# Top-16 attention on one Trainium2 core: the sixteen largest of a row found by way of fifteen groups, with one pool of two accumulator banks and another order of the loop

## The chip, the cores and the metric

The kernel runs on one core of one Trainium2 chip. The time is the device time of one execution in microseconds (us). Three runs of the kernel before gave 1539.97, 1541.5 and 1545.21 us; the median is 1541.5 us. Durations below come from one further execution, which was profiled.

The core has five engines that run their own instruction streams in order and wait for each other by semaphores: PE (matrix products, into PSUM banks), DVE (VectorE), ACT (ScalarE), POOL (GpSimd) and SP, which starts DMAs.

## What is computed

The reference is a small graph network on 1250 nodes with 512 channels: a graph layer, an attention with experts, a second graph layer, and a second attention. Each adds to the node features. Only the second attention is touched here. Cut to what matters, for each of 8 heads (m = 1250 rows, 64 channels a head):

```python
logits = jnp.einsum('bmd,bpd->bmp', q * scale, k)   # 8 x 1250 x 1250
_, idx = lax.top_k(logits, 16)                      # the sixteen largest of each row
attn = softmax(logits at idx)                       # over these sixteen alone
out = attn @ (v at idx)                             # then the output product wo
```

Each row of 1250 scores needs its sixteen largest. The kernel gathers nothing. It finds the sixteenth largest score of each row, forms exp of all scores, and multiplies by the sign of (score minus a limit just under the sixteenth). The negative products are later cut off at zero, so only the sixteen remain.

## The kernel before: how the second attention is staged

The 1250 rows are ten row tiles of P = 125 rows. A step n is one row tile i and one pair j of heads; a_ = 0 or 1 says which head of the pair. So there are 40 steps, four to a row tile, and 80 heads-of-a-tile, called heads below. The whole loop is recorded with a schedule written out by hand: each helper puts its instructions at the end of its engine's stream, and the order of the calls is the order on each engine. A semaphore wait is added wherever a tile is read or reused.

What a head goes through, with the lines of the kernel before:

- `scores1` (L1592): six matmuls write the score tile S of 125 x 1250 float32. S takes three PSUM banks, and each of the two heads of a pair has one S (two pools of three banks). The next step's matmuls for the same a_ wait until the S of this step has been read for the last time.
- `first1` (L1606 to L1609): DVE's MAX8 instruction gives the eight largest of S. POOL then makes nm (minus the largest) and gap (a small distance), by three one-column instructions.
- `without1` (L1617): DVE's MATCH_REPLACE8, with the load of its eight values, copies S to `rest` in SBUF with those eight put out.
- `second1` (L1626, L1627): MAX8 over `rest` gives the ninth to the sixteenth, and POOL makes `below`, the limit, with one more one-column instruction.
- `weights1` (L1634): ACT writes e = exp(S + nm). `select1` (L1641, L1644): ACT writes the sign sg of (S + below), with a sum over the row, and POOL multiplies e by sg in place. This multiplication of 125 x 1250 elements is called **the product** below; both of its inputs are in SBUF. The sign is the last reader of S.
- One step later `turn1` (L1654) and `keep1` (L1661): five groups of four transposes on PE into a PSUM bank, each copied by ACT to SBUF with negative values cut to zero.
- Two steps later `values1` (L1710), `outputs1` (L1720): forty small matmuls with the values v, and ACT's copy of the result.
- By row tile: `halves1` splits the next tile's queries (ACT L1577, POOL L1578, two DMAs on SP), in two of the four steps. `sums1`, `sums_exp1`, `sums_over1`, `sums_wide1`, `sums_turn1`, `sums_keep1` and `scale1` form the sums of the sixteen exponentials and scale the output of the tile before (POOL L1670, L1684 and L1698 among them). `project1` (L1728) and `finish1` (L1736, L1738) are the output product, the addition to the node features and the DMA out.

PSUM has eight banks here: six for the two S, one for the transposes (pool ps_t1) and one for everything else that PE writes (pool ps_o1).

At the end the row sums of the signs are compared with N - 32. If a row did not select exactly sixteen, the whole result is computed again by a slower general program that stands behind it.

Of the kernel before, what the change touches and what calls it, by code (L numbers as in the profile page):

```python
# [9 lines left out]
F32 = mybir.dt.float32  # L10
# [562 lines left out]
def tile_usual(ctx: ExitStack, tc: tile.TileContext, a: dict, out: bass.AP):  # L573
# [968 lines left out]


    TINY = 2.0 ** -22
    wo_pool, wo_p = pool("wo", 1)
    w_o = wo_p.tile([128, K, D], F32, name="w_o1")
# [3 lines left out]
    with (  # L1550
        tc.tile_pool(name="att1", bufs=2, side="right", reuse_waits="tile") as at1,
        tc.tile_pool(name="ps_t1", bufs=1, space=PSUM) as ps_t1,
        tc.tile_pool(name="ps_o1", bufs=1, space=PSUM) as ps_o1,
        tc.tile_pool(name="ps_s1b", bufs=1, space=PSUM) as ps_s1b,
        tc.tile_pool(name="ps_s1a", bufs=1, space=PSUM) as ps_s1a,
    ):
        ps_s1 = (ps_s1a, ps_s1b)
        w_v = at1.tile([128, K, D], F32, name="w_v1b", bufs=1)
        v_b = at1.tile([P, D], F32, name="v_b1b", bufs=1)
        signs = at1.tile([P, T * H], F32, name="signs", bufs=1)  # L1560
        steps = [(i, j) for i in range(T) for j in range(K)]
        last = len(steps) - 1
        score, found, bests, es, pTs, outs, turned = {}, {}, {}, {}, {}, {}, {}

# [17 lines left out]
        def scores1(n, a_, *chunks):  # L1582
            if n > last:
                return
            i, j = steps[n]
            h = 2 * j + a_
            if (n, a_) not in score:
                score[n, a_] = ps_s1[a_].tile([P, 3 * 512], F32, name="S")
            for c in chunks:
                n0, n1 = c * 512, min(c * 512 + 512, N)  # L1590
                for x in range(2):
                    nc.tensor.matmul(score[n, a_][:, n0:n1], stacks[i][:, x, h, :], K2[:, h, n0:n1],  # L1592
                                     start=(x == 0), stop=(x == 1))


        def first1(n, a_):
            if n > last:
                return
            i, j = steps[n]
            h = 2 * j + a_  # L1600
            if h == 0:
                bests[i] = at1.tile([P, H, TOPK], F32, name="best")
            top = bests[i][:, h, :]
            nm = at1.tile([P, 1], F32, tag=f"nm{a_}", name="nm1")
            gap = at1.tile([P, 1], F32, tag=f"gap{a_}", name="gap")
            nc.vector.max(out=top[:, 0:8], in_=score[n, a_][:, :N])  # L1606
            nc.gpsimd.tensor_scalar(nm, top[:, 0:1], -1.0, None, op0=ALU.mult)
            nc.gpsimd.tensor_scalar(gap, top[:, 7:8], -1.0, top[:, 0:1], op0=ALU.mult, op1=ALU.max)
            nc.gpsimd.tensor_scalar(gap, gap, TINY, None, op0=ALU.mult)  # L1609
            found[n, a_] = (nm, gap, top)  # L1610

        def without1(n, a_):
            if n > last:
                return
            nm, gap, top = found[n, a_]
            rest = at1.tile([P, N], F32, name="rest", bufs=1)
            nc.vector.match_replace(out=rest, in_to_replace=top[:, 0:8], in_values=score[n, a_][:, :N],  # L1617
                                    imm_value=LOWEST)
            found[n, a_] = (nm, gap, top, rest)

        def second1(n, a_):
            if n > last:
                return
            nm, gap, top, rest = found[n, a_]
            below = at1.tile([P, 1], F32, tag=f"below{a_}", name="below")
            nc.vector.max(out=top[:, 8:16], in_=rest)  # L1626
            nc.gpsimd.tensor_scalar(below, top[:, 15:16], -1.0, gap, op0=ALU.mult, op1=ALU.add)  # L1627
            found[n, a_] = below

        def weights1(n, a_):  # L1630
            if n > last:
                return
            e = at1.tile([P, N], F32, tag=f"e{a_}", name="e")
            nc.scalar.activation(e, score[n, a_][:, :N], AF.Exp, bias=found[n, a_][0])  # L1634
            es[n, a_] = e

        def select1(n, a_):
            if not 0 <= n <= last:
                return
            sg = at1.tile([P, N], F16, tag=f"sg{a_}", name="sg", bufs=1)  # L1640
            nc.scalar.activation(sg, score.pop((n, a_))[:, :N], AF.Sign, bias=found.pop((n, a_)),  # L1641
                                 accum_out=signs[:, 2 * n + a_ : 2 * n + a_ + 1])
            e = es[n, a_]
            (nc.vector if 2 * n + a_ == 2 * last + 1 else nc.gpsimd).tensor_mul(e, e, sg)  # L1644

        def turn1(n, g):
            if not 0 <= n <= last:
                return
            if g == 0:
                pTs[n] = at1.tile([P, 2 * T, P], F32, name="pT1")  # L1650
            turned[n, g] = ps_t1.tile([128, 512], F32, tag="t", name="ps_t1")
            g0, g1 = GROUPS[g]
            for b in range(g0, g1):
                nc.tensor.transpose(turned[n, g][:P, span(b - g0, b - g0 + 1)],  # L1654
                                    es[n, b // T][:, span(b % T, b % T + 1)], ident[:P, :P])
# [31 lines left out]
        def sums_turn1(i):  # L1687
            turned[i] = ps_t1.tile([128, 512], F32, tag="t", name="ps_t1")
            rb = sums.pop(i)
# [10 lines left out]
        def values1(n, t0, t1):  # L1700
# [3 lines left out]
            if t0 == 0:  # L1704
                outs[n] = ps_o1.tile([128, 512], F32, tag="o", name="O")
            pT = pTs[n]
# [15 lines left out]
        def project1(i, c, width=D // K, y=None):  # L1722

            if y is None:
                y = ps_o1.tile([128, 512], F32, tag="o", name="O")[:P, :width]
            cols = slice(c * width, (c + 1) * width)
# [14 lines left out]
        def values_late1(t):  # L1741
            ps = ps_o1.tile([128, 512], F32, tag="o", name="ps_v1")
            value_product1(ps[:P], t, w_v)
            lates.append((t, ps))
# [6 lines left out]
        def signs_over1():  # L1751
# [5 lines left out]
            nc.vector.tensor_copy(worst[:, 1:2], edges)  # L1757
            ps = ps_o1.tile([128, 512], F32, tag="o", name="ps_w1")[:1, :2]
            nc.tensor.matmul(ps, ones, worst, start=True, stop=True)
# [7 lines left out]
        with tc.manual_schedule():  # L1767
            nc.sync.dma_start(w_v, a["qkv"][:, 2 * D :].rearrange("(k p) f -> p k f", p=128))
            nc.sync.dma_start(v_b, bass.AP(tensor=a["v_b"].tensor, offset=a["v_b"].offset, ap=[[0, P], [1, D]]))
            for a_ in range(2):  # L1770
                halves1(0, a_)
            scores1(0, 0, 2, 0, 1)
            for n in range(len(steps)):


                i, c = n // K - 1, n % K
                if i >= 0 and c == 1:
                    sums_over1(i)
                first1(n, 0)
                values1(n - 2, 0, 5)  # L1780
                select1(n - 1, 1)
                turn1(n - 1, 0)
                values1(n - 2, 5, 8)
                keep1(n - 1, 0)
                without1(n, 0)
                if n == 1:
                    keep_late1()
                scores1(n, 1, 2, 1, 0)
                if n < 2:
                    values_late1(T - 3 + 2 * n)  # L1790
                if n <= last and c < 2:
                    halves1(steps[n][0] + 1, c)
                weights1(n, 0)
                turn1(n - 1, 1)
                values1(n - 2, 8, T)
                keep1(n - 1, 1)
                second1(n, 0)
                outputs1(n - 2)
                if i >= 0:
                    if c == 0:  # L1800
                        sums1(i)
                    if c == 1:
                        sums_wide1(i)
                    if c == 2:
                        sums_turn1(i)
                        sums_keep1(i)
                    if c == 3:
                        scale1(i)
                first1(n, 1)
                select1(n, 0)  # L1810
                turn1(n - 1, 2)
                if i >= 1:
                    project1(i - 1, c)
                scores1(n + 1, 0, 2)
                keep1(n - 1, 2)
                if i >= 0 and c == 0:
                    sums_exp1(i)
                if n == 0:
                    keep_late1()
                without1(n, 1)  # L1820
                turn1(n - 1, 3)
                keep1(n - 1, 3)
                scores1(n + 1, 0, 0, 1)
                if n == 0:
                    values_late1(T - 2)
                weights1(n, 1)
                turn1(n - 1, 4)
                keep1(n - 1, 4)
                second1(n, 1)
                if n == 1:  # L1830
                    keep_late1()
                finish1()

# [6 lines left out]
            turn1(n - 1, 0)  # L1840
            values1(n - 2, 5, 8)
            keep1(n - 1, 0)
            sums_exp1(i)
            turn1(n - 1, 1)
            values1(n - 2, 8, T)
            keep1(n - 1, 1)
            outputs1(n - 2)
            sums_over1(i)
# [92 lines left out]
```

## Time and profile before

| What | Value |
|---|---|
| median of three runs | 1541.5 us |
| the profiled execution's own time | 1539.01 us |
| its span in the trace | 1537.1 us |
| first and last MAX8 over S (L1606) | start at 1109.4 and 1506.0 us |
| length of four steps (one row tile), L1606 at 1271.53 to 1311.92 us | 40.39 us |
| busy in the span: PE, DVE, ACT, POOL | 1431.5, 898.1, 707.3, 424.8 us |

The span is the time from the first to the last recorded instruction; the execution's own time is 1.9 us longer. Busy time is the time in which an engine worked on an instruction; matmuls are pipelined and their ends are modelled, so a busy PE is not a PE at its peak. Engine times in a row of groups are the duration of one instruction on its engine. An instruction can begin before the one ahead of it on the same engine has ended, so the distance from start to start can be shorter than the duration.

### The profile page before, as it was taken

To read this page: it belongs to the slowest core of one execution; us is meant where nothing else is said; L and a number is where in the kernel's file an instruction comes from. 1 tells how busy PE (TensorE), PEld (TensorE's weight loads), DVE (VectorE), ACT (ScalarE), POOL (GpSimd) and SP (SyncE) were. 2 spreads that over 40 slices of the span, in tenths; PEclk is the share of its full clock that TensorE was granted. 3 is DMA by queue.
4 is the path that set the end of the run, shared out by engine and by line. 5 is a ranking of instruction groups with operands and counts; after the bars stand their busy time and mean duration, and the time that the engine had idled before them with its cause. 6 is when DMAs were issued, how large, how long until landed. Compare 5 with 4: busy or idle time off the path is not lost.

```text
span 1537.1 us, 21430 instructions
## 1 busy us (share of the span) xinstructions
PE 1431.5 (93%) x8127; PEld 934.1 (61%) x8127; DVE 898.1 (58%) x1412; ACT 707.3 (46%) x1351; POOL 424.8 (28%) x621
## 2 busy tenths in 40 slices
PE   6999999978999998999999999989888999999997
PEld 4557744457778766444444446654466777777775
DVE  8895567544443332422222435653588998999894
ACT  3333444455555552210000223431278888888884
POOL 1110000011111120000000112210168787887873
PEclk9999999989999999999999999999999999999999
DMA  4001000010101010200001100000200000000000
GB/s 138 29 1 55 1 0 1 6 46 14 42 18 48 22 26 17 79 28 28 28 28 41 42 28 1 5 23 0 78 11 14 14 22 21 22 21 22 21 8 23
DMA packets 42323, 41.12 MB, mean 27 GB/s; under 512 B 25738, under 2 KB 30084, under 8 KB 42211
## 3 DMA queue, kind: packets, MB, share of 16 engines
q1 hardware_dynamic: 42211, 39.66, 8.9%
q8 instruction: 66, 1.08, 0.3%
q14 instruction: 46, 0.38, 0.1%
HBM read 26.81 MB, written 2.56 MB: 19 GB/s over the span
## 4 chain that ended last, share of the span: by engine, by line
PE 69%; DVE 13%; ACT 11%; issue 3%; POOL 2%; DMA 0%; ACTq 0%; SPq 0%; DVEq 0%; POOLq 0%
PE ps_o L1334 9%; PE ps_mm L1326 7%; PE S L1592 5%; PE ps_mm L865 5%; PE ps_t L1654 5%; PE ps_mm L800 5%; PE S L1034 4%; PE ps_mm L1462 4%; PE ps_o L870 4%; PE ps_t L1122 4%; PE O L1143 3%; PE O L1710 3%; ACT sg L1641 3%; PE bank L768 2%; PE O L1187 2%
## 5 line engine op out<-in xcount | busy, mean ns | idle before, releaser
L1644 POOL TENSOR_TENSOR e<-e,sg 125x1250 f32<-125x1250 f32 x79 | 203.5, 2576 | 35.0 <-ACT sg L1641 34.1
L1336 DVE SCALAR_TENSOR_TENSOR X<-ps_o,gate,X 125x512 f32<-125x512 f32 x80 | 60.0, 750 | 177.0 <-PE ps_o L1334 177.0
L1592 PE MATMUL S<-K,stacks 128*125 128x512 f32 (+1 forms) x480 | 123.9, 382 | 29.6 <-ACT sg L1641 25.4
L1654 PE MATMUL ps_t<-ident,e 125*125 125x125 f32 x800 | 132.3, 288 | 11.8 <-ACT R L1695 6.7
L1334 PE MATMUL ps_o<-we,hid 128*125 128x512 f32 x320 | 141.2, 595 | 0.0
L1661 ACT ACTIVATE pT<-ps_t 125x500 f32<-125x500 f32 x200 | 118.1, 590 | 50.1 <-PE ps_t L1654 49.2
L1606 DVE MAX8 best<-S 125x8 f32<-125x1250 f32 x80 | 117.0, 1462 | 32.9 <-PE S L1592 32.0
L1654 PEld LDWEIGHTS ps_t<-ident,e 125*125 125x125 f32 x800 | 105.6, 187 | 47.9 <-ACT pT L1661 27.4
L1329 ACT ACTIVATE hid<-ps_mm,b 128x500 f32<-128x500 f32 (+1 forms) x40 | 24.6, 615 | 209.0 <-PE ps_mm L1326 209.0
L1626 DVE MAX8 best<-rest 125x8 f32<-125x1250 f32 x80 | 117.1, 1464 | 2.7
L1617 DVE MATCH_REPLACE8 rest<-best,S 125x1250 f32<-125x1250 f32 x80 | 116.0, 1450 | 0.0
L1326 PE MATMUL ps_mm<-yT,we 128*128 128x500 f32 (+1 forms) x320 | 115.8, 520 | 0.0
L1641 ACT ACTIVATE sg<-S,below 125x1250 f16<-125x1250 f32 x80 | 104.9, 1311 | 17.5 <-POOL below L1627 17.5
L1710 PE MATMUL O<-pT,yT 125*64 125x125 f32 x1600 | 111.8, 277 | 0.0
L1592 PEld LDWEIGHTS S<-K,stacks 128*125 128x125 f32 x480 | 75.3, 190 | 51.0 <-ACT sg L1641 31.8
L1634 ACT ACTIVATE e<-S,nm 125x1250 f32<-125x1250 f32 x80 | 104.1, 1302 | 2.7 <-DVE rest L1617 1.6
L1334 PEld LDWEIGHTS ps_o<-we,hid 128*125 128x125 f32 x320 | 59.0, 187 | 72.4 <-issue 69.6
L1005 POOL TENSOR_TENSOR stacks<-yT,stacks 64x125 fp32r<-64x125 f32 x80 | 34.3, 428 | 232.1 <-ACT stacks L1004 228.7
L1127 ACT COPY pT<-ps_t 125x500 f32<-125x500 f32 (+3 forms) x112 | 54.8, 489 | 92.7 <-PE ps_t L1122 91.8
L1326 PEld LDWEIGHTS ps_mm<-yT,we 128*128 128x128 f32 x320 | 60.2, 189 | 55.2 <-issue 53.3
L1383 POOL TENSOR_TENSOR X<-X,beta 125x512 f32<-125x512 f32 x10 | 13.1, 1315 | 289.9 <-DVE h L644 289.9
L1710 PEld LDWEIGHTS O<-pT,yT 125*64 125x64 f32 x1600 | 83.8, 136 | 14.6 <-DVE bad L1764 0.8
(240 smaller groups left out, 2656.7 us busy)
## 6 DMA issues: line engine op xcount, KB each, us to landing
we<-in_W SPq DMA_DIRECT2D x16, 512.0 KB
stacks<-stacks SPq DMA_DIRECT2D x160, 31.2 KB
stacks<-stacks SPq DMA_DIRECT2D x40, 125.0 KB
X<-in_x SPq DMA_DIRECT2D x5, 500.0 KB
out<-y SPq DMA_DIRECT2D x10, 250.0 KB
w_n<-in_wn SPq DMA_DIRECT2D x1, 1024.0 KB
w_c<-in_wc SPq DMA_DIRECT2D x1, 1024.0 KB
w_q<-in_Wq SPq DMA_DIRECT2D x1, 1024.0 KB
```

Source lines behind the costliest of these rows:

```text
L1326: nc.tensor.matmul(ps[:, :n], w1[:, k, f * 128 : (f + 1) * 128], yT[:, k, span(t0, t1)], start=(k == 0), stop=(k == K - 1))
L1334: nc.tensor.matmul(ps[:P], hid[:, f, span(t, t + 1)], w2[:, f, :], start=(f == 0), stop=(f == FF // 128 - 1))
L1592: nc.tensor.matmul(score[n, a_][:, n0:n1], stacks[i][:, x, h, :], K2[:, h, n0:n1], start=(x == 0), stop=(x == 1))
L1606: nc.vector.max(out=top[:, 0:8], in_=score[n, a_][:, :N])
L1617: nc.vector.match_replace(out=rest, in_to_replace=top[:, 0:8], in_values=score[n, a_][:, :N], imm_value=LOWEST)
L1626: nc.vector.max(out=top[:, 8:16], in_=rest)
L1634: nc.scalar.activation(e, score[n, a_][:, :N], AF.Exp, bias=found[n, a_][0])
L1641: nc.scalar.activation(sg, score.pop((n, a_))[:, :N], AF.Sign, bias=found.pop((n, a_)), accum_out=signs[:, 2 * n + a_ : 2 * n + a_ + 1])
L1644: (nc.vector if 2 * n + a_ == 2 * last + 1 else nc.gpsimd).tensor_mul(e, e, sg)
L1654: nc.tensor.transpose(turned[n, g][:P, span(b - g0, b - g0 + 1)], es[n, b // T][:, span(b % T, b % T + 1)], ident[:P, :P])
L1661: nc.scalar.activation(pTs[n][:, g0:g1, :], turned.pop((n, g))[:P, : (g1 - g0) * P].rearrange("p (t n) -> p t n", n=P), AF.Relu)
L1710: nc.tensor.matmul(outs[n][a_ * DH : (a_ + 1) * DH, :P], V[:, t, h * DH : (h + 1) * DH], pT[:, a_ * T + t, :], start=(t == 0), stop=(t == ...
```

## The change

Three things are changed, all in the second attention.

1. **The search.** Fifteen MAX8 instructions take the place of the one over S: twelve over every twelfth of the scores 0 to 1023, and three over every third of the scores 1024 to 1249 (parts 0 and 1 of `largest1`). Each gives the eight largest of its group, so `largest` holds 120 candidates in SBUF. `first1` takes the eight largest of the 120; `second1` puts them out with MATCH_REPLACE8 over 120 and takes the next eight. If one group held more than eight of the sixteen, the row would come out wrong and the general program would run.
2. **The small instructions.** nm, gap and below, which were POOL's, are DVE's now. nm is a tensor_scalar; gap and below are each one scalar_tensor_tensor on one column, with two inputs in SBUF.
3. **Banks and order.** The pools ps_t1 and ps_o1 of one bank each become one pool of two banks, which transposes, output tiles and output products use in turn. The calls in the loop stand in another order; among others the forty matmuls of `values1` follow each other without a gap.

```diff
+    SEARCHED = ((0, 1024, 12), (1024, N, 3))
+    FOUND = sum(x[2] for x in SEARCHED) * 8
...
-        tc.tile_pool(name="ps_t1", bufs=1, space=PSUM) as ps_t1,
-        tc.tile_pool(name="ps_o1", bufs=1, space=PSUM) as ps_o1,
+        tc.tile_pool(name="ps_to1", bufs=2, space=PSUM) as ps_to1,
...
+        PIECES = (((0, 512), (512, 1024), (1024, N)),) * 2
...
+        def largest1(n, a_, part):
+            if (n, a_) not in largest:
+                largest[n, a_] = at1.tile([P, FOUND], F32, tag=f"largest{a_}", name="largest")
+            n0, n1, step = SEARCHED[part]
+            for k in range(step):
+                c = part * SEARCHED[0][2] + k
+                nc.vector.max(out=largest[n, a_][:, 8 * c : 8 * c + 8], in_=score[n, a_][:, n0 + k : n1 : step])
+
         def first1(n, a_):
...
-            gap = at1.tile([P, 1], F32, tag=f"gap{a_}", name="gap")
-            nc.vector.max(out=top[:, 0:8], in_=score[n, a_][:, :N])
-            nc.gpsimd.tensor_scalar(nm, top[:, 0:1], -1.0, None, op0=ALU.mult)
-            nc.gpsimd.tensor_scalar(gap, top[:, 7:8], -1.0, top[:, 0:1], op0=ALU.mult, op1=ALU.max)
-            nc.gpsimd.tensor_scalar(gap, gap, TINY, None, op0=ALU.mult)
+            nc.vector.max(out=top[:, 0:8], in_=largest[n, a_])
+            nc.vector.tensor_scalar(nm, top[:, 0:1], -1.0, None, op0=ALU.mult)
...
-        def without1(n, a_):
...
         def second1(n, a_):
...
-            nc.vector.max(out=top[:, 8:16], in_=rest)
-            nc.gpsimd.tensor_scalar(below, top[:, 15:16], -1.0, gap, op0=ALU.mult, op1=ALU.add)
+            rest = at1.tile([P, FOUND], F32, name="rest")
+            nc.vector.match_replace(out=rest, in_to_replace=top[:, 0:8],
+                                    in_values=largest.pop((n, a_)), imm_value=LOWEST)
+            nc.vector.scalar_tensor_tensor(gap, top[:, 7:8], -1.0, top[:, 0:1], op0=ALU.mult, op1=ALU.max)
+            nc.vector.max(out=top[:, 8:16], in_=rest)
+            nc.vector.scalar_tensor_tensor(below, gap, TINY, top[:, 15:16], op0=ALU.mult, op1=ALU.subtract)
```

The loop's order before and after (the calls by row tile and those that act only in the first two steps are left out):

```
before: first1(n,0) values1(n-2,0,5) select1(n-1,1) turn1(n-1,0) values1(n-2,5,8) keep1(n-1,0)
        without1(n,0) scores1(n,1) halves1 weights1(n,0) turn1(n-1,1) values1(n-2,8,T) keep1(n-1,1)
        second1(n,0) outputs1(n-2) first1(n,1) select1(n,0) turn1(n-1,2) project1
        scores1(n+1,0: third piece) keep1(n-1,2) without1(n,1) turn1, keep1(n-1,3)
        scores1(n+1,0: first, second) weights1(n,1) turn1, keep1(n-1,4) second1(n,1) finish1

after:  largest1(n,0,1) select1(n-1,1) values1(n-2, all) outputs1(n-2) largest1(n,0,0) first1(n,0)
        turn1(n-1,0) second1(n,0) keep1(n-1,0) scores1(n,1) largest1(n,1,0) turn1(n-1,1) project1
        weights1(n,0) keep1(n-1,1) finish1 largest1(n,1,1) select1(n,0) turn1(n-1,2) first1(n,1)
        turn1(n-1,3) keep1(n-1,2) scores1(n+1,0: second, third) keep1(n-1,3) second1(n,1)
        scores1(n+1,0: first) turn1(n-1,4) halves1 weights1(n,1) keep1(n-1,4)
```

By row tile, after: POOL's `sums1` and `scale1` stand at the head of a step, ahead of the product of the head before; `halves1` and `sums_wide1` stand at its end.

## The prediction

> **What bounds the kernel now.** I read the busy time by engine in the stretch of the loop first, then the chain of work that ended last within one step, then the instructions in order of time, then the rows of single groups.
>
> ```profile
> 1109.30:1506.10 396.80, 360.64 (x3062) 285.74 (x3061) 359.54 (x369) 325.98 (x499) 312.37 (x437) 0.99 0.07 17
> ```
>
> These are length, PE, PEld, DVE, ACT, POOL, clock and DMA of the loop. 396.8 us are 39.5 steps of 10.04 us. DVE is busy for 91% of them, POOL for 79%, and the granted clock is 0.99. No engine is full, so a ring of waits must set the step. The chain inside one step shows it:
>
> ```profile
> 1284.49 1.08 POOL e L1644
> ...
> 1285.57 1.54 issue
> ...
> 1287.14 1.26 POOL stacks L1578
> ...
> 1288.49 0.28 POOL below L1627
> ...
> 1288.80 1.40 ACT sg L1641 x2
> ...
> 1290.24 0.47 PE S L1592 x2
> ```
>
> Columns are start, length and work; the first two rows together are one product, 1284.49 to 1287.07. The limit below (L1627) is queued on POOL behind a product (L1644) and whatever follows it; ACT's sign waits for below, and the scores wait for the sign. So from one product to the next: product, below, sign, product. In the rows: product 2.58, below 0.27, sign with its accumulator read 1.4, and two or three waits of about 0.1, which makes 4.4 to 4.5 us a head; ACT's other work ahead of the sign and POOL's other operations make up the rest to 5.02.
>
> **The search on DVE.** DVE spends this on a head before:
>
> ```profile
> 1302.65 1.47 DVE L1606 MAX8 best<-S 125x8 f32<-125x1250 f32 x1 [1.11 <-PE S L1592]
> 1304.15 0.09 DVE L1617 MATCH_VALUE_LOAD rest<-best,S 125x8 f32 x1
> 1304.23 1.45 DVE L1617 MATCH_REPLACE8 rest<-best,S 125x1250 f32<-125x1250 f32 x1
> 1305.71 1.46 DVE L1626 MAX8 best<-rest 125x8 f32<-125x1250 f32 x1
> 1307.09 1.46 DVE L1606 MAX8 best<-S 125x8 f32<-125x1250 f32 x1
> ```
>
> That is 4.44 us from head to head. The last two rows also show that an independent instruction starts 1.38 us behind a MAX8 of 1.46: 0.08 is saved. No short MAX8 is in the trace; the reductions over S (L1091) come in ten lengths and give the price of length:
>
> ```profile
> L1091 DVE TENSOR_REDUCE nm<-S 125x1 f32<-125x1250 f32 x8 | 11.3, 1450 | 0.0
> ...
> L1091 DVE TENSOR_REDUCE nm<-S 125x1 f32<-125x125 f32 x8 | 2.3, 283 | 5.8 <-ACT e L1101 5.8
> ```
>
> (1450 - 283) / 1125 = 1.037 ns an element and 153 ns besides; MAX8's 1462 ns at 1250 puts its fixed part at 165. A group of 85 scores then takes 254 ns, one of 75 243, and 120 candidates 290. Fifteen in a row, less 0.085 each: 12 x 0.169 + 3 x 0.158 = 2.50 us. Then come the end of the last (0.12), MAX8 over 120 with its wait (0.32), nm (0.07), value load (0.08), MATCH_REPLACE8 over 120 with its wait (0.31), the next MAX8 with its wait (0.32), below (0.07): 1.29. A head costs 3.79 us in place of 4.44, a step 7.8 with L1736 in place of 9.1, if nothing holds DVE up. Bounds for a group: 0.09 (length alone) to 0.254 (no overlap); at 0.254 a head is 5.1. I take 0.169, since every independent neighbour in these rows overlaps by about 0.085.
>
> The groups are read with a step of 12 scores, 48 bytes, from PSUM. ACT reads PSUM with a step of 10 scores at L776 in 578 ns for 500 elements; without a step L795 takes 576 for 500. I take no penalty. [...]
>
> The two parts do not overlap the scores: in the built order one wait, on the last of the six matmuls, stands ahead of all fifteen MAX8.
>
> **POOL and PE.** POOL loses 0.215 + 0.293 + 0.213 + 0.267 = 0.99 us a head, and below no longer waits in its queue. The forty matmuls in one block save PE about 0.4 us a step: 1.22 + 0.80 + 0.6 in three blocks, against 40 x 0.051 + 0.2. The two banks free PE from waiting for each keep1; for this project1's bank must be emptied by L1736, now between groups 12 and 13 on DVE. All of this is in the walks below. After the loop, the end loses next to nothing.
>
> **What the moved instructions wait for.** gap and below are now DVE instructions with two inputs in SBUF. The loop before has no such instruction on DVE (L1736 reads one input from PSUM). Just ahead of the loop there are two, beside POOL:
>
> ```profile
> 1102.15 2.73 POOL L1578 TENSOR_TENSOR stacks<-qT,stacks 64x500 fp32r<-64x500 f32 x2 [90.30 <-ACT stacks L1577]
> 1102.22 1.72 DVE L1530 TENSOR_TENSOR X<-X,wo_b 125x512 f32<-125x512 f32 x1
> ```
>
> L1530 takes 0.68 alone and 1.72 here. L1454, another scalar_tensor_tensor, starts at 983.53 inside a POOL operation that ends at 983.82, and ends 0.27 later with 250 elements; at 1010.68 with 500 it ends 0.54 after POOL does. So it starts over when POOL is done, and only the leftover scales with length. With one input it is otherwise: L638, one column, takes 0.14 inside a POOL operation, so nm is free. For one column with two inputs there is no row beside POOL. Low end: 0.16, as L1421 takes alone. High end: the whole rest of a product, up to 2.58. I take the high end, because the three blocked rows have the same kind of inputs, and the length did not change the blocking. [...]
>
> What is queued behind a blocked gap: the second MAX8, below, and the next head's fifteen MAX8; ACT's sign waits for below.
>
> **The sum.** I laid out the four steps of a row tile in the built order, each instruction starting when its engine is free and its wait is over, with these durations and waits of 0.1. The kernel before comes out at 40.5 us for 40.39 measured.
>
> Blocked: product 2.58, gap 0.07, MAX8 0.36, below 0.28 with its way to ACT, sign 1.39, way to POOL 0.14: 4.82 a head. DVE reaches the next gap 3.4 us after below, before the product ends (4.1), so every head is caught. Eight heads at 4.85 are 38.8. On top: 0.65 where halves1's cast and exp stand ahead of the sign on ACT, 0.8 where halves1's subtraction (1.24) holds below up, 1.2 where scale1 (1.25) stands between a product and gap, 0.3 for sums1: 41.75 us, 1.35 more than before. Ten row tiles: +13.5. The profiled execution's 1539.01 becomes 1552.5; the median, 2.5 above it, becomes 1555. Bounds of this case: 8 x 4.82 = 38.6 (all else hidden, -18) and 38.8 + 4.74 (all of POOL's other work exposed, +31). Inside these I expect 1540 to 1570.
>
> **Rivals.**
> 1. *Faster: one column passes POOL.* If gap and below cost 0.16 however busy POOL is, the ring is DVE's. The same layout gives 8.3, 9.1, 10.1 and 8.8 us for the four steps, 36.3 a tile: -41 us, 1500. For it: L638 and L1421. Against it: the blocked rows. It decides as soon as less than three quarters of the blocking remain: (40.4 - 36.3) / (41.75 - 36.3) = 0.75.
> 2. *Much slower: a group costs the high end.* At 0.254, because of the step through PSUM or for want of overlap, DVE needs 5.1 us a head: 10.5 a step, +24 us alone and +56 together with the blocking, 1565 to 1597. L776 and the overlap rows speak against it.
> 3. *It does not do what it says.* A row with more than eight of its sixteen in one group starts the general program, which repeats the whole work; no row prices it, but it is far outside the range. From the reference's inputs I count at most eight (one row of 10,000). Chance 0.01.
>
> **How the numbers follow.** Blocked 0.60 (slower 0.48, same 0.04, faster 0.08), free 0.31, nearly all of it faster, dear groups 0.08, mostly slower, general program 0.01. Faster 0.39, same 0.05, slower 0.56; 0.3% (4.6 us) is about what a measurement of this kernel can tell from no change. The likeliest is 1555, alone 1540 to 1570. Both signs hold much, so the range is 1494 to 1573, with about a tenth left out at each end.
>
> **What would show it.** In the profile after: MAX8 of 85 scores starting every 0.17 us (0.25 if I am wrong on the groups); one-column scalar_tensor_tensor of 1 to 2 us ending with a product (0.16 if rival 1 holds); products 4.8 to 5.9 us apart; DVE busy for most of the loop, much of it in gap and below. A gap of 0.16 beside a running product would make the forecast wrong.

## The result, and the profile after

The kernel before took 1541.8 us (median of ten runs), the changed kernel 1546.66 us (median of ten, 1544.82 to 1549.03). The ratio is 1.0034 with a 95% interval of 1.0025 to 1.0043: **slower by 5 us, where 13 us were forecast.** The waits that the forecast named are there, the size was not right, and the direction came out right by luck: it rests on the granted clock, which the forecast left out. With the clock full the changed kernel is 0.2% faster than the kernel before (experiment 8).

The loop of the changed kernel, in the columns of the first view of the prediction:

```profile
1110.20:1516.90 406.70, 350.98 (x3083) 299.79 (x3083) 385.59 (x1805) 330.73 (x505) 242.00 (x124) 0.96 0.07 17
```

DVE is busy for 95% of it, POOL for 60% (79% before), and the granted clock is 0.96, where it was 0.99 before. The 3% of clock look harmless; they turn out to be more than the whole difference.

Two heads in the chain of waits (start, length, work):

```profile
1276.43 0.15 DVE nm L1616
...
1276.83 2.11 DVE gap L1626
1278.95 0.21 DVE best L1627
...
1279.25 0.16 DVE below L1628
1279.41 1.85 DVE largest L1606 x12
...
1282.72 1.14 DVE gap L1626
...
1284.15 0.92 DVE below L1628
1285.07 2.29 DVE largest L1606 x15
```

POOL's products stood on this chain before; now gap and below stand on it, two instructions on one column that take up to 2.35 and 2.24 us. What POOL does in the same stretch (start, length, engine, line, operation):

```profile
1276.35 2.58 POOL L1644 TENSOR_TENSOR e<-e,sg 125x1250 f32<-125x1250 f32 x1 [2.71 <-ACT sg L1641]
1281.27 2.57 POOL L1644 TENSOR_TENSOR e<-e,sg 125x1250 f32<-125x1250 f32 x1 [2.33 <-ACT sg L1641]
1283.80 1.25 POOL L1582 TENSOR_TENSOR stacks<-qT,stacks 64x500 fp32r<-64x500 f32 x1
```

The first gap ends at 1278.94, the product beside it at 1278.93. The second ends at 1283.86, the product at 1283.84. The second below ends at 1285.07, the subtraction of halves1 at 1285.05. So each ends with the POOL operation beside it, and not before. nm, one column with one input, lies inside a product and takes its usual time. In the rows of single lines (shortest, median and longest, ns):

```profile
L1626 DVE SCALAR_TENSOR_TENSOR gap<-best x80: 149/1127/2354, 1113.3 to 1517.9; 125x1 f32<-125x1 f32 x80
L1616 DVE TENSOR_SCALAR nm<-best x80: 153/154/157, 1113.0 to 1517.6; 125x1 f32<-125x1 f32 x80
```

The search itself is a little cheaper than I had worked out:

```profile
L1606 DVE MAX8 largest<-S 125x8 f32<-125x85 f32 x640 | 104.2, 233 | 0.0
```

233 ns for one, where I had 254, and fifteen take 2.29 us in the chain above, 0.153 from start to start, where I had 0.169.

### The profile page after: what moved, and what is told of

Same layout as the page of the kernel before. It is cut to its first block, busy times and chain, and to the rows that moved or that the text cites. A ratio compares the mean times of both kernels' runs of the same rounds, so it can differ in the third digit from the quotient of the medians.

```text
span 1543.9 us, 22523 instructions
## 1 busy us (share of the span) xinstructions
PE 1419.9 (92%) x8127; PEld 947.3 (61%) x8127; DVE 922.0 (60%) x2852; ACT 708.8 (46%) x1351; POOL 350.8 (23%) x301
## 4 chain that ended last, share of the span: by engine, by line
PE 59%; DVE 29%; ACT 8%; issue 2%; DMA 0%; POOL 0%; DVEq 0%; ACTq 0%; SPq 0%
DVE largest L1606 9%; PE ps_o L1334 9%; PE ps_mm L1326 7%; PE ps_mm L865 5%; PE ps_mm L800 4%; DVE gap L1626 4%; PE S L1034 4%; PE ps_mm L1462 4%; PE ps_o L870 4%; PE ps_t L1122 4%; PE O L1143 3%; PE bank L768 2%; PE O L1187 2%; DVE below L1628 2%; PE S L1157 1%
## 5 line engine op out<-in xcount | busy, mean ns | idle before, releaser
L1606 DVE MAX8 largest<-S 125x8 f32<-125x85 f32 (+3 forms) x1200 | 191.8, 232 | 5.7 <-PE S L1596 5.6
L1654 PE MATMUL ps_t<-ident,e 125*125 125x125 f32 x800 | 135.3, 294 | 48.7 <-ACT pT L1661 37.3
L1654 PEld LDWEIGHTS ps_t<-ident,e 125*125 125x125 f32 x800 | 110.1, 194 | 75.6 <-ACT pT L1661 48.0
L1596 PE MATMUL S<-K,stacks 128*125 128x512 f32 x480 | 121.6, 389 | 11.4 <-ACT sg L1641 7.2
L1710 PE MATMUL O<-pT,yT 125*64 125x125 f32 x1600 | 101.0, 280 | 0.0
L1596 PEld LDWEIGHTS S<-K,stacks 128*125 128x125 f32 x480 | 81.6, 199 | 26.2 <-ACT sg L1641 9.8
L1710 PEld LDWEIGHTS O<-pT,yT 125*64 125x64 f32 x1600 | 90.5, 141 | 6.9 <-issue 1.3
L1626 DVE SCALAR_TENSOR_TENSOR gap<-best 125x1 f32<-125x1 f32 x80 | 93.9, 1174 | 0.0
L1034 PE MATMUL S<-K,stacks 128*125 128x512 f32 (+10 forms) x288 | 84.2, 400 | 7.1 <-ACT e L1101 6.6
L1122 PE MATMUL ps_t<-ident,e 125*125 125x125 f32 x440 | 81.5, 296 | 9.5 <-ACT pT L1127 6.0
```

What stands on the lines that cost most here:

```text
L1034: nc.tensor.matmul(ps[:, n0:w], stacks[n][:, x, a_, :], K2[:, 2 * j + a_, n0:w], start=(x == 0), stop=(x == 1))
L1122: nc.tensor.transpose(ps[:P, span(t - t0, t - t0 + 1)], es[n, a_][:, span(t, t + 1)], ident[:P, :P])
L1606: nc.vector.max(out=largest[n, a_][:, 8 * c : 8 * c + 8], in_=score[n, a_][:, n0 + k : n1 : step])
L1626: nc.vector.scalar_tensor_tensor(gap, top[:, 7:8], -1.0, top[:, 0:1], op0=ALU.mult, op1=ALU.max)
L1710: nc.tensor.matmul(outs[n][a_ * DH : (a_ + 1) * DH, :P], V[:, t, h * DH : (h + 1) * DH], pT[:, a_ * T + t, :], start=(t == 0), stop=(t == ...
```

## The experiments

The theory after the first look: the time of a head runs from product to product over the end of the blocked gap, below and the sign. The first rival: DVE is simply full, and a long gap only shows where its slack lies. The second: a blocked instruction costs little, and what costs is the later first maximum, or the order. All ratios are to the kernel before, with 95% intervals.

**1. One SBUF input in place of two** (`one_input`).

```diff
-nc.vector.scalar_tensor_tensor(gap, top[:, 7:8], -1.0, top[:, 0:1], op0=ALU.mult, op1=ALU.max)
+nc.vector.tensor_scalar(gap, top[:, 7:8], -1.0, top[:, 0:1], op0=ALU.mult, op1=ALU.max)
+nc.vector.tensor_scalar(gap, gap, TINY, None, op0=ALU.mult)
...
-nc.vector.scalar_tensor_tensor(below, gap, TINY, top[:, 15:16], op0=ALU.mult, op1=ALU.subtract)
+nc.vector.tensor_scalar(below, top[:, 15:16], -1.0, gap, op0=ALU.mult, op1=ALU.add)
```

> The changed kernel with gap and below written so that each has one tensor input in SBUF and its other value as a per-partition scalar operand; TINY gets an instruction of its own. All three stay on DVE. Theory (a DVE instruction with two tensor inputs in SBUF waits for the end of a running POOL operation): gap, TINY and below take 0.15 us each beside a running product, the 104 us of blocked time on DVE are gone, and a row tile goes from 41.05 to 35.2 to 35.8 us: 1488 to 1505 us. Rival (the blocking comes with any second value from SBUF, a scalar operand too): gap and below still end with a product, 1535 to 1550 us. Rival (DVE is full and gap only shows where the time is left over): the same idle time turns up elsewhere, 1535 to 1550 us, with a short gap.

Measured: 1514.36 us, 0.9821 (0.9805 to 0.9838). One more instruction on DVE for each head, and 32 us less than the changed kernel. Not all of it is the block: the clock of this kernel is at 1.00 from 1121 to 1505 us, and by experiment 8 about 8 of the 32 us are the clock's. Gap in this kernel:

```profile
L1626 DVE TENSOR_SCALAR gap<-best x80: 202/204/208, 1112.2 to 1484.2; 125x1 f32<-125x1 f32 x80
```

Not one of the 80 is blocked: with its second value as a scalar operand from SBUF gap takes 202 to 208 ns, also where it starts inside a product (at 1271.02 us in one from 1270.83 to 1273.41); with that value as a second tensor input it took 149 to 2354 ns in the changed kernel. The gain is smaller than I expected (1488 to 1505), because a row tile takes 37.8 us and not 35.5. What is late next stands in the chain of this kernel:

```profile
1273.52 1.28 ACT sg L1642 x2
1274.81 0.49 ACT pT L1662
...
1275.33 0.70 PE ps_t L1655 x4
1276.03 1.16 PE S L1596 x6
...
1277.63 2.60 PE O L1711 x40
```

DVE has only 4.3% of this chain between 1268 and 1310 us. PE waits for ACT's copy to empty one of the two banks, ACT does the sign ahead of that copy, and the scores stand behind the transposes.

**2. The limits back on POOL** (`limits_pool`), nm stays on DVE.

```diff
-nc.vector.scalar_tensor_tensor(gap, top[:, 7:8], -1.0, top[:, 0:1], op0=ALU.mult, op1=ALU.max)
+nc.gpsimd.tensor_scalar(gap, top[:, 7:8], -1.0, top[:, 0:1], op0=ALU.mult, op1=ALU.max)
+nc.gpsimd.tensor_scalar(gap, gap, TINY, None, op0=ALU.mult)
...
-nc.vector.scalar_tensor_tensor(below, gap, TINY, top[:, 15:16], op0=ALU.mult, op1=ALU.subtract)
+nc.gpsimd.tensor_scalar(below, top[:, 15:16], -1.0, gap, op0=ALU.mult, op1=ALU.add)
```

> The changed kernel with gap, TINY and below back on POOL as in the kernel before; nm stays on DVE; search, banks and order stay. Theory: below stands in POOL's queue behind the product again, so the ring is product, below, sign, product, as before: 39.5 to 40.7 us a row tile, 1533 to 1548 us, although DVE is busy for little more than 3 us a head. Rival (the shorter search and the order are worth their saving once the blocking is gone): 1495 to 1510 us.

Measured: 1551.95 us, 1.0061 (1.0044 to 1.0079), 4 us above what I had expected. The clock accounts for most of these 4: it is halved at six places between 1124 and 1524 us, and from 1205 us on a row tile takes 40.7 us without such a place and 41.8 to 41.9 us with one (three tiles). The chain shows the whole ring:

```profile
1273.02 2.57 POOL e L1645
1275.59 0.28 POOL gap L1626
...
1275.96 0.21 POOL gap L1627
...
1276.27 0.27 POOL below L1629
...
1276.56 1.40 ACT sg L1642 x2
...
1278.04 2.57 POOL e L1645
```

All three now stand behind the product, as DVE is early: 5.02 us from product to product. On POOL the limits wait in the queue, on DVE in the two-input form they wait for the same product by way of its block. That is why the change moved so little.

**3. Gap moved next to below** (`gap_late`).

```diff
-nc.vector.scalar_tensor_tensor(gap, top[:, 7:8], -1.0, top[:, 0:1], op0=ALU.mult, op1=ALU.max)
 nc.vector.max(out=top[:, 8:16], in_=rest)
+nc.vector.scalar_tensor_tensor(gap, top[:, 7:8], -1.0, top[:, 0:1], op0=ALU.mult, op1=ALU.max)
 nc.vector.scalar_tensor_tensor(below, gap, TINY, top[:, 15:16], op0=ALU.mult, op1=ALU.subtract)
```

> The changed kernel with gap moved behind the second MAX8, next to below; nothing else. Theory (ring: end of the product, what DVE does from gap to below, sign, product): after the product's end DVE has gap and below left in place of gap, MAX8 and below, 0.16 to 0.3 us less for each of 80 heads: 1522 to 1534 us. Rival (DVE is the bound by its total work, the blocked time is slack): same work, 1544 to 1549 us.

Measured: 1532.42 us, 0.9932 (0.9914 to 0.995), 14 us less than the changed kernel. From the end of gap to the end of below it is now 0.26 us in place of 0.46. But an undisturbed head falls only from 4.62 to about 4.5, since ACT is not free any sooner, and this kernel's clock is not halved once between 1124 and 1526 us. Experiment 8 shows that the clock alone is worth 8 us, so about 6 of the 14 are left for the shorter ring; at full clock a row tile takes 39.4 to 39.8 us here and 40.07 in experiment 8. The number was expected, half of its reason was not.

**4. Only the limits moved, in the kernel before** (`before_limits_dve`): the changed kernel's forms, with the long search, the banks and the order of before.

```diff
-nc.gpsimd.tensor_scalar(nm, top[:, 0:1], -1.0, None, op0=ALU.mult)
-nc.gpsimd.tensor_scalar(gap, top[:, 7:8], -1.0, top[:, 0:1], op0=ALU.mult, op1=ALU.max)
-nc.gpsimd.tensor_scalar(gap, gap, TINY, None, op0=ALU.mult)
+nc.vector.tensor_scalar(nm, top[:, 0:1], -1.0, None, op0=ALU.mult)
+nc.vector.scalar_tensor_tensor(gap, top[:, 7:8], -1.0, top[:, 0:1], op0=ALU.mult, op1=ALU.max)
...
-nc.gpsimd.tensor_scalar(below, top[:, 15:16], -1.0, gap, op0=ALU.mult, op1=ALU.add)
+nc.vector.scalar_tensor_tensor(below, gap, TINY, top[:, 15:16], op0=ALU.mult, op1=ALU.subtract)
```

> The kernel before (its search over 1250 scores, its banks, its order) with nm, gap and below on DVE in the changed kernel's forms, gap and below with two tensor inputs in SBUF. Theory (the blocked ring sets the time, not the search): about the kernel before, 39.4 to 40.2 us a row tile in the same layout, 1528 to 1541 us. Rival (the short search is what pays for the blocking in the changed kernel): DVE has 4.44 us of search and the blocking on top, over 5.3 us a head, 1560 us and more.

Measured: 1600.44 us, 1.0372 (1.0351 to 1.0392). Here my theory failed and the rival held. DVE is busy for 430.5 of 450 us, the blocked time counted in: gap takes 0.62 and below 0.41 us on average in place of 0.15, which with nm and the 4.44 us of search makes 5.6 us a head. With the long search DVE has no room for the block. So the short search does pay for something: it makes the room in which gap can wait. Experiment 7 has the short search and the blocked limits in the same banks and order and takes 30 us less. The clock has a part in this, too: it is halved at ten places of this loop and at one in experiment 7; how large a part was not measured.

**5. Only the limits moved, without the block** (`before_one_input`): the four small instructions of the kernel before as they are, on DVE.

```diff
...
-nc.gpsimd.tensor_scalar(gap, top[:, 7:8], -1.0, top[:, 0:1], op0=ALU.mult, op1=ALU.max)
+nc.vector.tensor_scalar(gap, top[:, 7:8], -1.0, top[:, 0:1], op0=ALU.mult, op1=ALU.max)
...
```

> The kernel before, its search, banks and order, with nm, gap, TINY and below on DVE, each with one tensor input in SBUF. Theory (the long search and the limits together fill DVE: 4.8 to 5.0 us a head as in the kernel before with blocked limits, less the blocked time): 40 to 41.5 us a row tile, 1538 to 1556 us, so neither part gains alone. Rival (the place of the limits alone is what the one-input version gained): 1508 to 1522 us.

Measured: 1565.13 us, 1.0147 (1.012 to 1.0174), more than expected, but on the theory's side. The chain is DVE alone:

```profile
1274.83 1.45 DVE rest L1617
...
1276.30 1.47 DVE best L1626
...
1277.87 0.21 DVE below L1627
1278.09 1.38 DVE best L1606
```

**6. Only the groups** (`search_only`): the fifteen MAX8 in the kernel before; nm, gap and below stay on POOL. MATCH_REPLACE8 and the second MAX8 go over the 120 candidates here, too.

```diff
-nc.vector.max(out=top[:, 0:8], in_=score[n, a_][:, :N])
+for n0, n1, step in SEARCHED:
+    for k in range(step):
+        nc.vector.max(out=largest[:, 8 * c : 8 * c + 8], in_=score[n, a_][:, n0 + k : n1 : step])
+        c += 1
+nc.vector.max(out=top[:, 0:8], in_=largest)
...
```

> The kernel before with the fifteen groups alone; nm, gap, TINY and below stay on POOL, banks and order stay. Theory (the product's ring sets the time, and the small instructions that POOL has to do ahead of the next product wait for the first maximum): the total search is shorter, but the first maximum comes later, 2.35 + 0.3 us behind the scores in place of 1.46, and nm and gap stand in POOL's queue ahead of the product; so no gain, and up to 1.2 us a head lost where that wait is open: 1545 to 1575 us. Rival (DVE's search is the bound of the kernel before): 0.65 us a head less, 1490 to 1515 us.

Measured: 1578.45 us, 1.0244 (1.0213 to 1.0274), with DVE busy for only 63% of the loop. What it costs stands in POOL's row for nm (after the bar: busy us, mean ns, and the idle time before it):

```profile
L1615 POOL TENSOR_SCALAR nm<-best 125x1 f32<-125x1 f32 x80 | 17.1, 214 | 104.4 <-DVE best L1614 104.4
```

In the kernel before POOL waits 43.4 us there. The groups shorten the whole search, but the first maximum comes 1.2 us later, and POOL cannot start the next product before it has done nm and gap. **Each part alone is a loss** (24 us for unblocked limits, 37 us for the groups); both together, without the block and in the new banks and order, are a gain of 27 us. The clock is halved in nine windows of this loop, one in nearly every row tile, so a part of the 37 us is the clock's; it was not separated. Unblocked limits and groups in the old banks and order were not run.

**7. The change in the old order and banks** (`old_order`): the edits of experiments 4 and 6 together.

> The fifteen groups and the limits on DVE as in the changed kernel, with the banks and the order of the kernel before. It tells what banks and order are worth inside the change. Theory (the ring of product, gap to below, sign is the same in both orders, and the forty matmuls in three blocks and two single banks make PE and ACT later): 1555 to 1575 us. Rival (banks and order are worth nothing while the blocked ring holds): 1544 to 1550 us.

Measured: 1570.28 us, 1.0183 (1.0158 to 1.0207). So banks and order are worth 24 us inside the change. Two things make the ring longer, and the reason that I gave (PE and ACT are later) is the larger of them. The first is in the chain:

```profile
1281.18 1.29 DVE gap L1616
1282.48 0.27 DVE rest L1624 x2
...
1282.77 0.30 DVE best L1633
...
1283.16 0.16 DVE below L1634
```

In the old order gap stands ahead of MATCH_REPLACE8, so that is left to do, too, when the product ends: 0.77 to 0.84 us from gap to below in place of 0.46. The second is one late sign in each row tile. ACT's operations ahead of it (start, length, engine, line, operation):

```profile
1309.88 0.26 ACT L1727 COPY oT<-O 128x125 f32<-128x125 f32 x1
1310.61 0.57 ACT L1702 COPY R<-ps_t 128x500 f32<-128x500 f32 x1 [0.47 <-PE ps_t L1698]
1311.09 1.31 ACT L1648 ACTIVATE sg<-S,below 125x1250 f16<-125x1250 f32 x1
```

Below had ended at 1309.43, 1.66 us before this sign. Ahead of the sign ACT had its copies to do and waited 0.47 us for PE's transposes of the sums. A row tile takes 42.64 us on average against 40.07 in experiment 8, at equal clock (six tiles from 1200 us on). Of these 2.57 us, 0.84 lie between the product and the end of below and 1.67 between below and the sign.

**8. The clock** (`after_again`, `warm`). In the changed kernel's row tiles I found 39.9 us and 41 to 42 us side by side. These are two neighbouring tiles; the third number from the end is the granted clock:

```profile
1276.30:1317.90 41.60, 36.08 (x338) 31.58 (x334) 39.70 (x179) 33.89 (x52) 25.31 (x14) 0.96 0.08 20
1317.90:1357.80 39.90, 34.18 (x328) 29.95 (x324) 38.15 (x183) 33.69 (x52) 25.05 (x13) 1.00 0.09 20
```

The clock is at 0.50 for 3.41 us at nine places between 1124 and 1521 us, whose distances are all multiples of 3.413 us, and at 1.00 between them. First, the same kernel once more:

> The changed kernel once more, for the granted clock. In its first profile the clock is halved for 3.41 us at nine places of the loop after 1120 us, on a fixed grid of 3.41 us, each time after a stretch in which PE was busy for about 0.6 or less; the heads beside them are 0.2 to 1.4 us late, 8.6 us together. The kernel before has no such place. Theory (the grid runs freely, and PE idles because of the blocked ring): again several halved windows, not all at the same heads, and a span of 1535 us plus about 1 us for each. Rival (the halved windows cost nothing, the late heads come from the program): the same heads late by the same time, wherever the windows fall.

One execution, 1547.64 us. Again nine places, two of them elsewhere against the heads. The first profile had one at 1374.0 us, the second has none there. The two stretches below each hold the same two heads, in the first profile and in the second:

```profile
1372.40:1384.20 11.80, 10.39 (x84) 9.10 (x84) 11.31 (x54) 9.23 (x15) 6.83 (x4) 0.86 0.10 23
```

```profile
1374.20:1384.70 10.50, 9.11 (x84) 7.91 (x84) 10.29 (x50) 9.00 (x15) 6.82 (x4) 1.00 0.11 26
```

The same work takes 1.3 us more with the halved window. The second profile has a window at 1396.2 us instead, and the two heads beside it take 10.9 us where the first profile has 9.5 at full clock. The lateness goes where the window goes. Ahead of the late sign ACT waits for PE. Its copy of `outputs1` in the first profile, with the halved window, and in the second:

```profile
1379.08 0.27 ACT L1720 COPY oT<-O 128x125 f32<-128x125 f32 x1 [1.07 <-PE O L1710]
```

```profile
1379.58 0.28 ACT L1720 COPY oT<-O 128x125 f32<-128x125 f32 x1
```

From below to the sign it is 1.68 us in this head of the first profile and 0.49 in the second. Then PE was kept busy:

```diff
-            for b in range(g0, g1):
+            for b in [x for _ in range(3 if g == 2 else 1) for x in range(g0, g1)]:
                 nc.tensor.transpose(turned[n, g][:P, span(b - g0, b - g0 + 1)],
```

> The changed kernel with the four transposes of the third group written three times into the same bank, the same values each time: 0.9 us more of PE work a step, ahead of a stretch in which PE idles for 1.1 to 1.2 us. Nothing waits on it that is not late anyway, as ACT does the sign before it reads this bank. Theory (windows of 3.41 us with PE busy for less than about 0.55 halve the clock in the next window, and that costs 8.6 us): PE's share in the poor windows rises by up to 0.26, none or one or two of the nine halved windows are left after 1120 us, all row tiles take about 40 us, and the time falls to 1536 to 1541 us in spite of more PE work. Rival (the halved windows are harmless): more PE work, 1545 to 1552 us.

Measured: 1539.01 us, 0.998 (0.997 to 0.999). **PE does eight more transposes a step, about 0.9 us (four take 0.43 to 0.44 us in the chains), and the kernel is 7.7 us faster than the changed kernel.** The loop from 1120 us on:

```profile
1120.00:1500.00 380.00, 356.87 (x3283) 311.83 (x3282) 360.62 (x1716) 318.01 (x486) 234.27 (x120) 1.00 0.08 18
```

No window is halved between 1124 and 1532 us, PE's poorest one there is busy for 0.75, and every row tile from 1200 us on takes 40.06 to 40.08 us. In the changed kernel the windows ahead of the halved ones were busy for 0.43 to 0.60; the poorest in the loop of the kernel before, from 1120 us on, is 0.56, and none is halved. Windows at 0.60 or less are 17 in the changed kernel and two in the kernel before.

**9. Neighbouring columns** (`adjacent`), one execution, on top of experiment 1.

```diff
-in_=score[n, a_][:, n0 + k : n1 : step]
+at = slice(n0 + 76 * k, min(n0 + 76 * k + 76, n1)) if part else slice(n0 + k, n1, step)
+in_=score[n, a_][:, at]
```

> The version with one SBUF input for the limits, with the three groups of the scores 1024 to 1249 cut into neighbours (76, 76 and 74 columns) in place of every third column. For the price of reading PSUM with a step. Theory (no penalty): the three MAX8 over neighbours take the same 0.22 us as with the step. Rival (a step through PSUM costs DVE a second cycle for each value): the neighbours take about 0.08 us less.

76 neighbouring scores take 233 ns and 74 take 225 (means); every third score took 239 for 76 and 225 for 75, every twelfth 234 for 85. So a step of 12 or 48 bytes costs a few ns at most, and not the 80 of the rival.

**10. One copy on DVE** (`keep_dve`): on top of experiment 1, the copy of the third group of transposes goes to DVE (`kept` is the bank's tile).

```diff
-nc.scalar.activation(pTs[n][:, g0:g1, :], kept, AF.Relu)
+if g == 2:
+    nc.vector.tensor_scalar(pTs[n][:, g0:g1, :], kept, 0.0, None, op0=ALU.max)
+else:
+    nc.scalar.activation(pTs[n][:, g0:g1, :], kept, AF.Relu)
```

> The version with one SBUF input for the limits, with one of the five copies of a step (keep1 of the third group, 500 columns from PSUM with the cut at zero) on DVE in place of ACT. In that version the chain runs through PE's transposes and matmuls and ACT's copies, exp and sign; ACT is busy for 87% of the loop and DVE for 81%. Theory (PE waits for ACT's copies in a ring over two banks): ACT loses 0.48 us a step and the sign is no longer ahead of this copy, 0.3 to 0.5 us a step less: 1494 to 1506 us. Rival (DVE's own work is now as late as ACT's): 1512 to 1525 us.

Measured: 1497.82 us, 0.9717 (0.97 to 0.9735). This is the fastest of all versions, 44 us below the kernel before. It agrees with the ring that experiment 1 left: two banks, emptied by ACT, which does the sign ahead of the copy. It also takes a copy a step off ACT, which was busy for 320.3 of 370 us there, so the ring and ACT's total work are not told apart.

## Why the prediction was right in what waits and wrong in its size

One row tile of the changed kernel with full clock (heads from 1317.9 us on), from product to product, in us. The product to the end of gap is 2.59, the sign 1.30 and its way to POOL 0.17 in every head:

| Head | gap's end to below's end | below to sign | sum | what is beside it |
|---|---|---|---|---|
| 0, 2, 6 | 0.46 | 0.10 | 4.62 | nothing |
| 1, 3 | 1.03, 1.33 | 0.30, 0.19 | 5.37, 5.58 | halves1 blocks below, its cast is ahead of the sign |
| 4 | 0.39 | 0.48 | 4.95 | ACT late |
| 5 | 1.21 | 0.09 | 5.36 | scale1 blocks below |
| 7 | 0.69 | 0.09 | 4.84 | sums1 blocks below |

The eight add up to 39.94.

- **What bounds the kernel before**: right. Experiments 2 and 6 show the ring over POOL's queue, and that a shorter search does nothing for it.
- **The search**: right within a tenth (0.153 in place of 0.169 a group), with no penalty for the step (experiment 9). What banks and order bring is on the ring (experiment 7): 0.84 us a tile up to the end of below, to which the place of gap behind MATCH_REPLACE8 belongs, and 1.67 us by which ACT comes to the sign earlier; what PE's 0.4 us a step do in this was not separated. The rival of dear groups did not come about; its price was too high besides, as 10.5 us a step are 42.0 a tile, 16 us more than before and not 24.
- **One column with two inputs is blocked, and every head is caught**: right, as 77 of the 80 gaps of the changed kernel start inside a product and end 11 to 21 ns behind it; the other three have no POOL operation beside them and take 149 to 153 ns. This was the choice of the high end, against rival 1. Experiment 1 shows that it decides between a gain of 27 us and none. Rival 1 had 41 there: the free layout had 36.3 us a tile, and PE and ACT hold it at 37.8.
- **The blocked head of 4.82 (4.85 in the sum)**: the first step that failed, a term that was too large. After gap I had MAX8 0.36 and below 0.28 with gap's own 0.07, 0.71 together; the trace has 0.46 + 0.10. For the sign and its way to POOL I had 1.53; it has 1.47. A head is 4.62 and not 4.85, and eight of these are 1.84 us a tile too much.
- **The extras of 2.95 us a tile**: right as a sum (3.0), wrong in the parts. halves1's subtraction costs 0.57 and 0.87, as it meets below twice a tile, where I had 0.8; scale1 meets below and not gap and costs 0.75 in place of 1.2; sums1 0.23 in place of 0.3; ACT 0.67 in place of 0.65.
- **The clock**: the second step that failed, a term that was missing. By the ring alone a tile is 39.94 us, against 40.24 from product to product in the kernel before, so it alone would have been a small gain of 3 us; experiment 8, with the clock full, is 0.2% below the kernel before. I named 0.99 as the clock and took it as given. With the blocked ring PE is idle more often (busy for 351.0 of the loop's 406.7 us, for 360.6 of 396.8 in the kernel before), if not longer at a stretch (up to 1.5 us from 1120 us on, up to 2.17 in the kernel before), and the nine halved windows cost 8.6 us by the late heads (1.1 to 1.5 us for each of six, less for the others). That turns -3 into +5.6; measured are +4.9.

The parts nearly close: -18.4 us for eighty heads, +0.3 for the extras, +8.6 for the clock and +1.5 for the base (40.24 us a tile where I had 40.39) make -8.0; the measurement lies 8.3 us below the forecast. So "slower" came out right by luck, as a sum of two errors: a ring that I made too long, and a clock that I left out.

## What to carry to other kernels

A small instruction with two tensor inputs in SBUF on DVE cost here what was left of the POOL operation beside it, up to 2.35 us, and with a scalar operand 0.20 to 0.21 us (experiment 1), so take that form; that one edit is 2% of the whole time, about a quarter of it by way of the clock. A shorter search is worth only what the ring around it lets through. When a change makes PE wait more often, read the granted clock window by window: a mean of 0.96 in place of 0.99 was more than the whole difference here.

## What was unexpected in the hardware

The granted clock of PE was halved for 3.41 us at a time, on a grid of 3.413 us that does not follow the row tiles of 39.9 to 41.9 us, after windows in which PE was busy for 0.43 to 0.60 of the time and never idle for more than 1.5 us at a stretch. That the grid runs free of the program these runs do not show, as seven of the nine halved windows met the same heads in both profiles. What brings a halved window about stays open. It is not a share of the window alone: in the same kernel windows busy for 0.53 to 0.59 were left alone as well, and in `limits_pool` PE was busy for 1.73 of the 4.00 us from 1338 us on and the clock stayed at 1.00 up to 1378. Nor is it the longest idle stretch alone: the loop of the kernel before has one of 2.17 us that ends at 1169.51 us, and no halved window from 1124 us to its end.
